# Where the weights of the second projections are split into high and low halves

## The chip, the cores and the metric

The kernel runs on one core of a Trainium2 chip. The metric is the device time of one launch in microseconds (us), median of several runs. The five engines of a core are named as in the profile: PE (TensorE, matrix products; PEld are its weight loads), DVE (VectorE), ACT (ScalarE), POOL (GpSimd) and SP (SyncE, which here issues nearly all transfers).

## The reference

One decoder layer on 8 sequences of 100 tokens, width 1024, all in float32, with a layer normalization after each of three parts:

```
x = layernorm(x + retention(x, Wq, Wk, Wv, Wg, Wo, g_norm_weight))
x = layernorm(x + attention(x, ctx_2048, wq, wk, wv, wo, wk_ctx, wv_ctx, q_norm_w, k_norm_w))
x = layernorm(x + w_down @ (silu(w_gate @ x) * (w_up @ x)))
```

The retention has 8 heads: queries and keys of 128, values and gates of 256, a decaying causal mask in place of a softmax. The attention has 16 query heads on 4 key and value heads of 128; its keys are 722 of the context and the 100 of the sequence itself. The part that the change is about are the second projections, those of the attention's own queries, keys and values:

```
q = rms_norm((x @ wq).reshape(B, L, 16, 128), q_norm_w)
k = rms_norm((x @ wk).reshape(B, L, 4, 128), k_norm_w)
v = (x @ wv).reshape(B, L, 4, 128)
q, k = rope(q), rope(k)
```

## The kernel before, in words

Activations lie with the features on the 128 partitions and the tokens along the free dimension, in two halves of N = 400 tokens (four sequences each). A float32 product is made of three products of float32r numbers: every operand is kept as a high half (a cast on ACT, L67) and a low half (operand minus high half, on DVE, L68), and `mm3` (L85) multiplies high by high, high by low and low by high. A weight tile covers 1024 inputs and 128 outputs: 512 KB raw, 1 MB as two halves.

`load_w` (L70) loads a raw weight into a tile `wst` (3 buffers), and splits it into a tile `w` (4 buffers). `load_ws` (L80) loads a weight that was split earlier: it reads both halves, 1 MB, out of the DRAM tensor `wcd` straight into a tile `w`, and needs neither `wst` nor a split. Both pools serve the whole kernel.

The stages, in order of time:

- The retention (to about 430 us). Head 0 is computed directly, heads 1 to 7 with seven products in place of eight (`seven`, L342). Each head has three units (queries and keys, values, gates), and `in_turn` (L408) interleaves the steps of neighbouring units. A unit loads two raw weights and takes three `w` tiles. After a head's value unit `after_v` (L552) puts the values in place and calls `core` (L475): scores, products with the values, and at its end one of the eight context weights `wc` is loaded, split, and written to `wcd` (L498 to L503), where the later stages find it. After the gate unit `after_g` (L557) calls `gated` (L505), which writes the head's result to the DRAM tensor `o1d`.
- The output projection of the retention, `out_proj` (L216), for one half of the tokens after the other, about 430 to 580 us. Before each half, eight loads of 800 KB bring `o1d` into four `big` tiles (L562), of which there are only four, so the second half's loads wait for the first half's products. It goes through eight blocks m of 128 outputs (in half 0 the first four together), each with two weights of `wo1` and 48 products. After the last block a layer normalization follows.
- The second projections, about 575 to 842 us (L622 to L654). For each of the four key heads kv there are six weights `w2[kv, i]`: four of queries (i = 0 to 3), one of keys (4), one of values (5). They are loaded by L628 with `load_w`, four or two at a time. Each is used for both halves, 24 products of 400 columns for each. A query or key result then passes, on ACT, POOL and DVE: square (L645), the all-reduce over partitions on POOL (L125), the rotation (L133 to L137), the inverse root (L113 to L120), the scaling (L650) and a split (L68), and goes to DRAM (L654). A value result is transposed by PE (L148) after a copy on ACT (L145). Between the weights the keys of the first context sequence are prepared (`context_keys`, L592, which loads from `wcd`).
- The attention over the eight sequences, its output projection, and the feed-forward part.

The accumulators are PSUM banks: three with tag a, four with tag s, one with tag v. PE executes in order. The order of the instructions on each engine is not written by hand: the launch builds the program with `schedule_with_timeline_sim=True` (L1070), by which a planner orders them from the program text, a simulated timeline, and the buffers that are free. SP issues its transfers in that order, each when what it waits for is done.

Of the kernel before, what the change touches and what calls it, by code (L numbers as in the profile page):

```python
# [9 lines left out]
FR = mybir.dt.float32r  # L10
# [6 lines left out]
P = 128  # L17
# [3 lines left out]
KT = D // P  # L21
QT = KT // 2
# [9 lines left out]
NKV = 4  # L32
# [7 lines left out]
def decoder_layer(ctx, tc, xT, cT, w1, wo1, w2, wo2, wc, w3, wd, gw, qw, kw, trig, dec, mask, out):  # L40
    nc = tc.nc
# [14 lines left out]
    def f32(ap):  # L56
        return ap.bitcast(F32)
# [19 lines left out]
            split(w[:, :, c], st[:, c])  # L77
        return w

    def load_ws(i):  # L80
        w = wp.tile([P, 2, KT * P], FR, tag="w", name="w", bufs=4)
        nc.sync.dma_start(out=f32(w), in_=f32(wcd[i]))
        return w

    def mm3(acc, lh, ll, rh, rl, start, stop, chain=False):  # L85
        nc.tensor.matmul(acc, lh, rh, start=start, stop=False, skip_group_check=chain)  # L86
# [70 lines left out]
    zd = dr.tile([2, P, KT, N], F32, name="zd")  # L157
    zd2 = dr.tile([2, P, KT, N], F32, name="zd2")
    wcd = dr.tile([2 * NKV, P, 2, KT * P], FR, name="wcd")
    hd = dr.tile([QT - 1, 7, P, 2, QT, N], FR, name="hd")  # L160
    h3d = dr.tile([4, P, 2, QT, N], FR, name="h3d")

# [50 lines left out]
        return dcy  # L213


    def out_proj(half, w, load_o, res, yp, ybufs, p, make_z, dst, after=None):  # L216

        og = load_o(half)
        y = yp.tile([P, KT, N], F32, tag="y", name="y", bufs=ybufs)
        s1 = p.tile([P, N], F32, tag="s1", name="s1", bufs=2)  # L220
        first = 4 if half == 0 else 1
        for ms in [range(first)] + [[m] for m in range(first, KT)]:
            if half == 1 and KT - 1 in ms:
                early = norm_early(y, s1, p)
            accs = [bank(("aaasaaaa", "sssaaass")[half][m])[:, :N] for m in ms]
            for c in range(2):
                for m, acc in zip(ms, accs):
                    wt = load_w(w[m, c])
                    for k in range(KT):
                        kt = c * KT + k  # L230
                        rh, rl = og(kt)
                        a = acc if len(rh.shape) == 2 else bt(acc)
                        mmw(a, wt, k, rh, rl, kt == 0, kt == 2 * KT - 1)
            for m, acc in zip(ms, accs):
                rs = yp.tile([P, N], F32, tag="rs", name="rs", bufs=2)
                nc.sync.dma_start(out=rs, in_=res[half, :, m])
                if half == 1 and m == KT - 1:
                    nc.vector.tensor_tensor(rs, rs, early[0], ALU.subtract)
                nc.vector.tensor_tensor(y[:, m], acc, rs, ALU.add)
                if half == 0 or m < KT - 1:  # L240
                    add_up(s1, y, m)
        z = make_z(half)
        if half == 0:
            scaled(y, norm_root(y, s1, p), lambda m: dst[half, :, m], z)
        else:
            norm_more(y, early, p, KT - 1)
            norm_late(y, early, p, lambda m: dst[half, :, m], z)
        if after is not None:
            after(half, y)
        return z  # L250
# [171 lines left out]
    with sbuf("l1", 2) as p:  # L422
# [127 lines left out]
                of_qk(half, i, acc)  # L550

        def after_v(h, c):  # L552
            for (half, blk), acc in c:
                of_v(half, blk, acc, (half, blk) == HB[3])
            core(h)

        def after_g(h, c):  # L557
            gated(h, {hb: silu(acc, None if hb == HB[3] else acc) for hb, acc in c})

        in_turn([unit(h, i, then) for h in range(1, NH1) for i, then in ((0, after_qk), (2, after_v), (4, after_g))])  # L560
# [6 lines left out]

    z1pool = sbuf("z1", 4)
    z1p = z1pool.__enter__()
    with sbuf("ln1", 1) as p:  # L570
        z1 = [out_proj(half, wo1, load_o1, xT, p, 2, p, lambda _: [z1p.tile([P, 2, QT, N], FR, tag="z", name="z")
                                                                 for _ in range(2)], zd) for half in range(2)]


    kapool = sbuf("ka", 2, "right")
# [16 lines left out]
    def context_keys(kv):  # L592

        kall = ka.tile([P, 2, SC + T], FR, tag="kall", name="kall")
        wk = load_ws(2 * kv)
        sq = ka.tile([P, SC], F32, tag="ksq", name="ksq", bufs=1)
        ss = ka.tile([P, 6 * P], F32, tag="kss", name="kss", bufs=1)
        row = dr.tile([6, P], F32, tag="row", name="row", bufs=2)
        nc.gpsimd.memset(ss[:, SC:], 1.0)

        def step(hf):
            n, at = SN[hf], slice(hf * SH, hf * SH + SN[hf])
            acc = proj(wk, cz[hf], n)
            nc.scalar.activation(sq[:, at], acc, AF.Square)  # L604
            nc.gpsimd.partition_all_reduce(ss[:, at], sq[:, at], P, RED.add)  # L605
            nc.scalar.activation(kall[:, 0, at], acc, AF.Copy, scale=kws)
            nc.vector.scalar_tensor_tensor(kall[:, 1, at], acc, kws, f32(kall[:, 0, at]), ALU.mult, ALU.subtract)
            if hf:
                nc.sync.dma_start(out=row.rearrange("c p -> (c p)")[None, :], in_=ss[0:1])
        return step, (kall, row)  # L610

    def context_values(kv):

        wv = load_ws(2 * kv + 1)
        vt = ka.tile([P, SC], F32, bufs=1, tag="cvt", name="cvt")
        for hf in range(2):
            copy = nc.scalar.copy if hf == 0 else nc.vector.tensor_copy
# [457 lines left out]
```

## Time and profile before

| | |
|---|---|
| median of 3 runs | 2516.4 us (2514.87 to 2523.12) |
| the profiled execution | 2517.7 us |
| its span, first to last instruction | 2515.9 us |
| PE busy | 2465.4 us |
| DVE busy | 1992.2 us |
| ACT busy | 1343.5 us |
| transfers | 433.96 MB, mean 172 GB/s |

The prediction quotes the page (busy time and share of each engine, then the span in 40 slices whose digits are tenths of busy time), the table by stretches of time, the list of who waited for whom (engine, tile and line that waited, the engine, tile and line that ended the wait, total us, times, longest), and the timeline (start and length in us, engine, line, operation, tiles; in brackets the idle time before it and what ended it). A tile is named by the program's name for it; "w<-wst" is an operation that writes w and reads wst. A line may be that of a helper: all splits of weights stand at L67 and L68. A wait is put down to the releaser that the profile saw last, which need not be the true one.

### The profile page before, as it was taken

The page shows a single profiled execution, that of the slowest core. Times are in us where ns is not written, and L with a number is a line of the kernel's source. Part 1 is how long each engine was busy: PE and PEld are TensorE (multiplying, and loading weights), DVE is VectorE, ACT ScalarE, POOL GpSimd, SP SyncE. Part 2 cuts the span into 40 slices and gives each one's busy share as a digit, 9 for nine tenths or more (in the row PEclk, how much of TensorE's full clock was granted, in tenths as well). Part 3 has the DMA queues.
Part 4 walks back from the last instruction along what each step waited for, and adds up shares of the span by engine and source line. Part 5 has one row for each costly group of instructions (what it writes and reads, how often), then busy time and mean ns, then how long its engine had stood idle before and what let it go on. Part 6 is the DMA issues. An engine that isn't in the chain of part 4 may idle for free.

```text
span 2515.9 us, 37158 instructions
## 1 busy us (share of the span) xinstructions
PE 2465.4 (98%) x14036; PEld 2442.0 (97%) x14036; DVE 1992.2 (79%) x3110; ACT 1343.5 (53%) x2264; POOL 481.2 (19%) x234
## 2 busy tenths in 40 slices
PE   8999999999899999999999999999999999999997
PEld 8999999999899999999999999999999999998997
DVE  7678876568989798899999999866987777666656
ACT  6667676335767565556566566533544544432221
POOL 0111111002645334433433433100000000000000
PEclk9999999999999999999999999999999999999999
DMA  7334445774444654554554554574455445388731
GB/s 240 110 110 127 136 144 187 239 266 148 144 152 133 207 175 142 178 166 151 169 176 144 166 192 135 189 273 152 145 181 192 159 160 167 127 302 311 250 102 53
DMA packets 224450, 433.96 MB, mean 172 GB/s; under 512 B 47338, under 2 KB 168042, under 8 KB 211854
## 3 DMA queue, kind: packets, MB, share of 16 engines
q1 hardware_dynamic: 223118, 427.39, 50.7%
q0 software_dynamic: 1152, 4.19, 1.1%
q8 instruction: 110, 1.80, 0.3%
q14 instruction: 70, 0.57, 0.1%
HBM read 322.18 MB, written 109.35 MB: 172 GB/s over the span
## 4 chain that ended last, share of the span: by engine, by line
PE 89%; DVE 6%; ACT 1%; DMA 1%; issue 1%; SPq 0%; DVEq 0%; ACTq 0%
PE a L88 18%; PE a L86 18%; PE a L87 18%; PE s L88 9%; PE s L87 9%; PE s L86 9%; PE v L88 2%; PE v L86 2%; PE v L87 2%; PE s L491 1%; PE s L688 1%; DVE r L120 1%; DVE r L119 1%; PE s L148 1%; DMA tp<-in_xT 1%
## 5 line engine op out<-in xcount | busy, mean ns | idle before, releaser
L86 PE MATMUL a<-big,w 128*128 128x400 f32 (+2 forms) x1808 | 611.4, 339 | 11.7 <-ACT big L67 7.4
L87 PE MATMUL a<-big,w 128*128 128x400 f32 (+2 forms) x1808 | 611.1, 338 | 0.0
L88 PE MATMUL a<-big,w 128*128 128x400 f32 (+2 forms) x1808 | 609.7, 338 | 0.0
L67 ACT CAST w<-wst 128x1024 fp32r<-128x1024 f32 (+1 forms) x231 | 239.2, 1038 | 389.4 <-PE s L88 130.7
L68 DVE TENSOR_TENSOR w<-wst,w 128x1024 fp32r<-128x1024 f32 (+1 forms) x231 | 281.0, 1218 | 117.0 <-ACT w L67 115.1
L86 PEld LDWEIGHTS a<-big,w 128*128 128x128 f32 x1808 | 341.3, 189 | 13.3 <-ACT big L67 7.7
L87 PEld LDWEIGHTS a<-big,w 128*128 128x128 f32 x1808 | 342.0, 189 | 1.3 <-DVE big L68 0.3
L88 PEld LDWEIGHTS a<-big,w 128*128 128x128 f32 x1808 | 342.0, 189 | 0.9 <-DVE w L68 0.2
L86 PE MATMUL s<-big,w 128*128 128x400 f32 x664 | 230.6, 347 | 0.1
L87 PE MATMUL s<-big,w 128*128 128x400 f32 x664 | 229.2, 345 | 0.0
L88 PE MATMUL s<-big,w 128*128 128x400 f32 x664 | 229.1, 346 | 0.0
L125 POOL PARTITION_ALL_REDUCE ss<-sq x56 | 161.1, 2881 | 336.3 <-DMA zd<-y 167.0
L605 POOL PARTITION_ALL_REDUCE kss<-ksq x64 | 173.2, 2706 | 116.4 <-ACT ksq L604 115.7
L86 PE MATMUL a<-z,w 128*128 128x400 f32 x488 | 168.6, 346 | 8.0 <-ACT r L118 4.3
L88 PE MATMUL a<-z,w 128*128 128x400 f32 x488 | 169.4, 348 | 0.7 <-DVE w L68 0.7
L87 PE MATMUL a<-z,w 128*128 128x400 f32 x488 | 169.4, 347 | 0.0
L87 PE MATMUL s<-z,w 128*128 128x400 f32 x400 | 139.1, 348 | 2.4 <-DVE z L68 2.4
L86 PE MATMUL s<-z,w 128*128 128x400 f32 x400 | 139.9, 350 | 0.0
L88 PE MATMUL s<-z,w 128*128 128x400 f32 x400 | 139.4, 348 | 0.0
L722 ACT ACTIVATE s<-s,rk 128x400 f32<-128x400 f32 x160 | 87.7, 591 | 91.9 <-DVE sm L742 65.5
L86 PEld LDWEIGHTS s<-big,w 128*128 128x128 f32 x664 | 124.6, 188 | 1.4 <-ACT w L67 0.4
L87 PEld LDWEIGHTS s<-big,w 128*128 128x128 f32 x664 | 124.6, 188 | 1.1
(330 smaller groups left out, 5650.9 us busy)
## 6 DMA issues: line engine op xcount, KB each, us to landing
wst<-in_w SPq DMA_DIRECT2D x135, 512.0 KB
w<-wcd SPq DMA_DIRECT2D x64, 1024.0 KB
wst<-in_wo SPq DMA_DIRECT2D x64, 512.0 KB
hd<-h SPq DMA_DIRECT2D x12, 1400.0 KB
wst<-in_wd SPq DMA_DIRECT2D x64, 256.0 KB
big<-o1d SPq DMA_DIRECT2D x16, 800.0 KB
qd<-d SPq DMA_DIRECT2D x32, 400.0 KB
q<-qd SPq DMA_DIRECT2D x32, 400.0 KB
```

The lines of the kernel that those rows point to most:

```text
L67: nc.scalar.copy(hi, src)
L68: nc.vector.tensor_tensor(lo, src, f32(hi), ALU.subtract)
L86: nc.tensor.matmul(acc, lh, rh, start=start, stop=False, skip_group_check=chain)
L87: nc.tensor.matmul(acc, lh, rl, start=False, stop=False, skip_group_check=chain)
L88: nc.tensor.matmul(acc, ll, rh, start=False, stop=stop, skip_group_check=chain)
L119: nc.vector.scalar_tensor_tensor(q, ss, eps, q, ALU.add, ALU.mult)
L120: nc.vector.scalar_tensor_tensor(q, q, 3.0, r, ALU.subtract, ALU.mult)
L125: nc.gpsimd.partition_all_reduce(y, x, P, op)
L148: nc.tensor.transpose(tr[0:T, b * P:(b + 1) * P], vt[:, b * T:(b + 1) * T], ident)
L491: nc.tensor.matmul(bt(o)[:, b], vv[:, b * P:(b + 1) * P], pf[:, b], start=True, stop=True)
L605: nc.gpsimd.partition_all_reduce(ss[:, at], sq[:, at], P, RED.add)
L722: nc.scalar.activation(sc, sp, AF.Copy, scale=rk[:, c:c + 1])
```

## The change

The 24 weights `w2[kv, i]` are no longer split where they are used. A new DRAM tensor `w2d` (24 MB) holds both halves of each. A new function `split_ahead` takes the next of them from a list, loads and splits it with `load_w`, and writes the 1 MB tile to `w2d`. It is called at the head of `after_v` and of `after_g` in the retention's heads 1 to 7 (14 calls), and in the retention's output projection by way of a new argument `beside` of `out_proj`, once after the products of each block: in half 0 for blocks 4 to 7 and in half 1 for blocks 0 to 5, until the list is empty (10 calls). The second projections read the halves with `load_ws`, which is given the source instead of an index.

```diff
-    def load_ws(i):
+    def load_ws(src):
         w = wp.tile([P, 2, KT * P], FR, tag="w", name="w", bufs=4)
-        nc.sync.dma_start(out=f32(w), in_=f32(wcd[i]))
+        nc.sync.dma_start(out=f32(w), in_=f32(src))
         return w
+
+    ahead = [(kv, i) for kv in range(NKV) for i in range(6)]
+
+    def split_ahead():
+
+        kv, i = ahead.pop(0)
+        nc.sync.dma_start(out=f32(w2d[kv, i]), in_=f32(load_w(w2[kv, i])))
...
+    w2d = dr.tile([NKV, 6, P, 2, KT * P], FR, name="w2d")
...
-    def out_proj(half, w, load_o, res, yp, ybufs, p, make_z, dst, after=None):
+    def out_proj(half, w, load_o, res, yp, ybufs, p, make_z, dst, after=None, beside=None):
...
                         mmw(a, wt, k, rh, rl, kt == 0, kt == 2 * KT - 1)
+            if beside is not None:
+                beside(half, ms[-1])
             for m, acc in zip(ms, accs):
...
         def after_v(h, c):
+            split_ahead()
             for (half, blk), acc in c:
...
         def after_g(h, c):
+            split_ahead()
             gated(h, {hb: silu(acc, None if hb == HB[3] else acc) for hb, acc in c})
...
+    def weights_ahead(half, m):
+        if ahead and (half == 1 or m >= QT):
+            split_ahead()
...
-        wk = load_ws(2 * kv)
+        wk = load_ws(wcd[2 * kv])
...
-        wv = load_ws(2 * kv + 1)
+        wv = load_ws(wcd[2 * kv + 1])
...
-                ws = [load_w(w2[kv, i]) for i in range(i0, i1)]
+                ws = [load_ws(w2d[kv, i]) for i in range(i0, i1)]
```

More of the change, by code (lines that the diff above doesn't have):

```diff
@@ L569, in decoder_layer @@
     z1p = z1pool.__enter__()
+    def weights_ahead(half, m):
+        if ahead and (half == 1 or m >= QT):
+            split_ahead()
     with sbuf("ln1", 1) as p:
         z1 = [out_proj(half, wo1, load_o1, xT, p, 2, p, lambda _: [z1p.tile([P, 2, QT, N], FR, tag="z", name="z")
-                                                                 for _ in range(2)], zd) for half in range(2)]
+                                                                 for _ in range(2)], zd, None, weights_ahead)
+              for half in range(2)]
     kapool = sbuf("ka", 2, "right")
```

## The prediction

> **What bounds the kernel now.** First the page: its busy shares, and its slices in time.
>
> ```profile
> PE 2465.4 (98%) x14036; PEld 2442.0 (97%) x14036; DVE 1992.2 (79%) x3110; ACT 1343.5 (53%) x2264; POOL 481.2 (19%) x234
> ...
> PE   8999999999899999999999999999999999999997
> DVE  7678876568989798899999999866987777666656
> ```
>
> TensorE (PE) does not idle for more than 51 us of 2515.9 us. A change that takes nothing from PE can win only where PE waits or runs slowly. So I read the table by stage next (columns: stretch, its length, busy time and number of instructions of PE, PEld, DVE, ACT and POOL, granted clock, DMA share, GB/s). The stretches are the retention, the output projection up to its second half, the load burst between the halves, the second half, the normalization and start of the second projections, and these in two parts.
>
> ```profile
> 110.00:430.00 320.00, 319.50 (x1919) 317.34 (x1919) 247.05 (x368) 219.23 (x350) 37.73 (x18) 1.00 0.43 137
> 430.00:504.00 74.00, 74.00 (x419) 74.00 (x419) 37.79 (x47) 30.11 (x39) 6.16 (x4) 1.00 0.75 240
> 504.00:530.00 26.00, 24.63 (x133) 23.74 (x132) 14.22 (x22) 9.47 (x15) 0.00 (x0) 1.00 0.93 368
> 530.00:575.00 45.00, 44.74 (x247) 44.41 (x246) 27.91 (x41) 15.86 (x22) 0.00 (x0) 1.00 0.61 188
> 575.00:616.00 41.00, 37.70 (x190) 36.17 (x191) 36.97 (x60) 23.74 (x42) 7.51 (x2) 0.96 0.51 157
> 616.00:720.00 104.00, 91.68 (x479) 89.55 (x479) 101.59 (x142) 73.59 (x142) 55.14 (x19) 0.95 0.42 136
> 720.00:842.00 122.00, 121.11 (x680) 120.34 (x679) 110.56 (x158) 87.16 (x167) 64.94 (x26) 1.00 0.46 157
> ```
>
> In the retention and the output projection PE is full and VectorE (DVE) is at 77% and about 55%. From 616 to 720 it is the reverse: DVE is busy 101.6 of 104 us, and PE does 479 instructions, where from 720 to 842 it does 680 in 122 us, 5.57 per us. At that rate 479 take 86 us, so **this stretch loses 18 us**: 12.3 us idle, the rest at a lowered clock and in stretched products. The same table for the DVE instructions on tile w alone gives the splits of the weights there (length, DVE busy and count):
>
> ```profile
> 616.00:720.00 104.00, 13.44 (x10) 0.95 0.42 136
> 720.00:842.00 122.00, 12.87 (x10) 1.00 0.46 157
> ```
>
> The list of what PE waited for between 604 and 720 (total, times, longest):
>
> ```profile
> PE a L86 <- ACT r L118: 4.3, 1, 4.3
> PE s L148 <- ACT vt L145: 3.5, 2, 2.8
> PE a L86 <- DMA w<-wcd: 2.5, 1, 2.5
> PE s L87 <- DVE z L68: 2.4, 1, 2.4
> PE a L86 <- ACT w L67: 1.4, 1, 1.4
> PE a L88 <- DVE w L68: 0.7, 1, 0.7
> ```
>
> The first is put down to ACT, but the timeline shows DVE's L135 read of an accumulator end at 635.3 us and PE go on at 635.44: all banks were full and DVE was behind. Four splits (at 617.7, 622.5, 625.1 and 631.6 us; the third took 2.51 us where others take 1.22) stand ahead of it on DVE. After this wait ten products come 0.33 us apart instead of 0.18. The waits for L145 are DVE's backlog as well: ACT copies vt only after casts that waited for DVE's L650. Two waits are for splits themselves, one is for a load, and one for the normalization's last split.
>
> **What is removed.** 24 splits (ACT cast 1.04 us, DVE subtraction 1.22 us each) leave the second projections: 4 before 590 us, 10 in the DVE-bound stretch, 10 after 720.
> - 616 to 720: DVE loses 13.4 us of 101.6 and comes to 88.2, against 86 us of PE work. Of PE's 18.1 us, the load wait at 677 stays (2.5 us idle and about 1.5 us of slow clock: eleven products at 0.30 apart). That leaves 14.1; DVE can give back 13.4. Both engines are then nearly level, so some waits must come back: I take 2 us off. **Gain 11.4 us**; bounds 2.1 us (only the two waits that name a split) and 18.1.
> - Before 616: PE waits 1.1 us at 575.9 for the cast of a w2 weight, which goes. Splits at 582.7 and 588.0 (2.45 us) stand in DVE's queue among the normalization's steps, and PE then waits 2.4 us for its z. I take half: 1.2 us. **Gain 2.3 us**; bounds 0 and 5.4 (1.1, 2.4 and 1.9 of slow clock).
> - After 720: DVE loses 12.9 us, but PE is busy 121.1 of 122. Gain nothing.
>
> **What is added: 14 pieces in the retention** (load 512 KB, cast, subtraction, write 1 MB; two in each of seven heads). A head takes 53 us. DVE gets 2.4 us more on about 41 and ACT 2.1 on 36, PE's 319.5 of 320 us cover both. Each piece also keeps a raw buffer (of 3) and a w buffer (of 4) until its write has landed. The nearest rows: the context weight that the head already splits and writes (cast at 261.05, second ACT copy at 264.62, write issued at 265.69, next DMA on it at 270.3: 9 us of a buffer), and in 110 to 430 PE waited 0.5 us in all. So nothing is the lower bound. For the upper: with one buffer held, three serve the products, and the scarcest weight has two products, 24 x 0.182 = 4.4 us, from release to use; cast and subtraction take 2.3 us, and the subtraction's wait for its cast was 27.9 us over 11 times between 160 and 420, so 2.5 us: 0.4 us late, times 14, 6 us. The nearest row says nothing, so I take **1.5 us**.
>
> On SP each write waits for its subtraction, and later raw loads, o1d stores and wc loads are queued behind it. The loads are issued early (five between 267 and 295), and ACT and DVE waited under 4 us for raw weights from 160 to 420, so I price this within the 1.5 us.
>
> **10 pieces in the output projection.** A block m takes 48 products, 8.7 us, and loads 1 MB of weights and 0.2 MB of residue; with 1.5 MB more it moves 2.7 MB, 310 GB/s, and the trace reaches 410 to 429 GB/s from 507 to 524 us. DVE and ACT have room (27.9 and 15.9 of 45 us). The tight place is the burst: 6.4 MB of o1d for the second half can be asked for only as the first half's tiles come free (issues from 504.45 to 511), and PE wants the last of them 8.7 us after 512.3. A piece's 1.5 MB is 3.7 us there. Bounds nothing and 5.4 us (3.7 and 1.7 of clock); I take **2 us**, since a part falls before the burst. The page "DMA: Bandwidth & Descriptors" of the Trainium skill (Queues, rings and completion order) has each DMA engine take the descriptors of one issuing queue in ring order. This speaks against the change: a write issued ahead of the o1d loads holds them all up. By it this term would be 3.7 us and not 2; no row here shows such a write.
>
> **1 MB loads in place of a 512 KB load and a split.** The row is the load at 677: issued on SP at 670.82, landed 6.2 us later.
>
> ```profile
> 670.82 0.38 SPq L82 DMA_DIRECT2D w<-wcd  x1
> ...
> 677.00 0.67 PE L86 MATMUL a<-big,w 128*128 128x362 f32 x1 [2.46 <-DMA w<-wcd]
> ```
>
> The second weight of a pair takes a buffer that comes free 4.4 us before the pair ahead ends, and is wanted 4.4 us into its own: 8.7 us against 6.2. It fits, unless SP is 2.5 us late. Bounds: nothing, and 8 us (two more waits of 4 us, at the other places where a key weight is wanted with a pair). I take **1 us**. The same page (Anatomy of one DMA) fits 2.0 us and bytes over 436 GB/s, an estimate of 4.4 us for 1 MB; the row has 6.2 with other traffic beside it, and by the page's figure this term would be nothing.
>
> **Sum.** 11.4 + 2.3 - 1.5 - 2 - 1 = 9.2 us. The profiled execution took 2517.7 us (span 2515.9 and 1.8 around it), so it would take 2508.5. The median of the three runs, 2516.4, lies 1.3 us lower: 2507.2, **2507 us**, 0.4% faster.
>
> **Rivals.**
> 1. *DVE's chain stays the bound.* All-reduces on POOL fill 52 of the 104 us, and DVE operations beside them stretch (L136 takes 0.56 us as a rule and up to 2.17). Without splits DVE still runs level with PE, and each stretched step delays a bank. For it: 88 against 86 us. Against: from 720 on the all-reduces are as dense (56.6 in 122 us), splits are there too, and PE is full. Half of the 11.4 us returns: 2516.4 - 5.7 - 2.3 + 4.5 = 2513 us.
> 2. *Slower: the w buffers of the retention.* At the end of each head's v unit a piece and the context weight come together and hold two of four buffers for 8 to 9 us. The product after them then waits: the longest wait of a subtraction for its cast is 5.8 us; with 2.3 less the 4.4 of cover, PE stops for 3.7. Times seven: 26 us, and 2516.4 - 13.7 + 3 + 26 = 2532; half of that, 13 us, gives 2519; the middle is 2525. It outweighs the gain from 1.5 us a head. Against: the heads' own PE work on scores (about 6 us) lies just there, and the same place now costs nothing.
> 3. *The loads take the place of the splits:* SP holds the 1 MB loads up behind stores that wait for DVE, and the waits of PE change only their name. 8 us instead of 1 there, 3.7 in the burst: 2516.4 - 13.7 + 1.5 + 3.7 + 8 = 2516 us; the change then does not do what it says.
>
> **Chances.** Forecast 0.55 (own range 2499 to 2512), rival 1 0.18, rival 2 0.15, rival 3 0.12. 0.3%, 7.5 us, is about what a measurement of this kernel can tell from no change. Of the forecast 0.45 lies below 2508.9 and 0.10 above; rival 1 gives 0.05 and 0.13; rival 3 counts as no change with 0.07 and as slower with 0.05; rival 2 is slower. So 0.50 faster, 0.30 the same, 0.20 slower. The range leaves 0.1 out at each side: 2498 (a gain of 18) to 2525.
>
> **What would show it.** In the profile after: the busy DVE share from the start of the second projections falls under nine tenths, the waits for L118 and L145 go, and the first 479 PE instructions there take some 90 us. Waits of PE for loads into w tell rival 3. The retention still takes 53 us a head; more, with PE waiting for w, is rival 2. PE waiting for big at the start of the second half is the burst. The forecast is wrong if PE's lost time in that stage stays above 9 us, or the retention and output projection lose more than 8.

## The result, and the profile after

The changed kernel takes **2543.2 us** (median of four runs, 2541.3 to 2545.0) against 2515.6 us for the kernel before on the same chip: a ratio of 1.0103, interval 1.0091 to 1.0115. It is 27.6 us slower, where 9.2 us faster was predicted. The profiled execution took 2543.8 us, with a span of 2542.0; that is 26.1 us over the span before.

The page after, busy time and slices:

```profile
PE 2474.5 (97%) x14036; PEld 2444.0 (96%) x14036; DVE 1992.4 (78%) x3110; ACT 1346.1 (53%) x2264; POOL 470.1 (18%) x234
...
PE   8999999889999999999999999999999999999997
DVE  7777777565987789989989989866987777666755
```

Each engine has exactly as many instructions as before, so the splits have only moved; the transfers grew from 434 to 484 MB. In PE's row the eight at the eleventh slice of before is a nine, and there are two new eights, slices 8 and 9 (445 to 572 us), where DVE has a five and a six. The time went where DVE was not the bound.

The table by stage after (columns as in the prediction; the stretches are the heads up to the scores of head 3, the heads from there to those of head 7, the last part of the retention with the first half of the output projection, and its second half):

```profile
112.00:213.00 101.00, 101.00 (x605) 100.66 (x605) 82.08 (x121) 70.28 (x113) 13.82 (x6) 1.00 0.53 171
213.00:445.00 232.00, 221.18 (x1295) 214.93 (x1293) 174.30 (x258) 155.25 (x244) 24.36 (x12) 0.99 0.57 189
445.00:542.50 97.50, 88.50 (x473) 85.53 (x473) 51.53 (x60) 39.92 (x49) 6.24 (x4) 0.96 0.89 310
542.50:620.00 77.50, 67.89 (x346) 65.30 (x344) 46.50 (x67) 29.25 (x40) 0.00 (x0) 0.94 0.92 334
```

The kernel before in stretches that answer to the last three, with about the same PE instructions:

```profile
213.00:430.00 217.00, 217.00 (x1311) 215.89 (x1311) 167.03 (x247) 149.83 (x240) 25.51 (x12) 1.00 0.45 144
430.00:514.00 84.00, 82.63 (x464) 82.04 (x464) 42.62 (x53) 32.35 (x42) 6.16 (x4) 1.00 0.77 253
514.00:578.00 64.00, 62.87 (x344) 61.95 (x343) 40.16 (x61) 24.08 (x35) 0.00 (x0) 1.00 0.67 230
```

From 112 to 213 us PE has no idle time in the new kernel, though three pieces are written in that stretch (at 127.6, 159.8 and 183.0 us). From 213 us on PE idles for 10.8 us where it did not idle at all, then for 9.0 where it was 1.4, then for 9.6 where it was 1.1, at a lower granted clock each time (0.99, 0.96 and 0.94 for 1.00).

The second projections after, cut at the same counts of PE instructions as before (the 190 ahead of the stretch that the prediction calls DVE-bound, its 479, and the rest):

```profile
618.13:654.00 35.87, 35.87 (x190) 34.70 (x191) 32.12 (x55) 20.78 (x38) 7.23 (x2) 1.00 0.65 224
654.00:748.00 94.00, 89.17 (x479) 88.30 (x478) 92.04 (x132) 64.76 (x132) 54.20 (x19) 0.96 0.56 201
748.00:876.80 128.80, 127.79 (x719) 126.95 (x718) 102.60 (x155) 81.30 (x164) 63.36 (x27) 1.00 0.59 209
```

Before, the middle part is the prediction's line from 616 to 720 us; the other two are:

```profile
576.30:616.00 39.70, 37.28 (x190) 35.74 (x189) 35.71 (x58) 22.92 (x41) 7.51 (x2) 0.96 0.51 156
720.00:850.50 130.50, 127.73 (x718) 126.66 (x716) 113.39 (x165) 89.16 (x173) 66.70 (x27) 1.00 0.50 164
```

So before they took 39.7, 104.0 and 130.5 us. The 479 instructions take 94 us, so 10 us are gained there. DVE is still busy 92 of these 94 us, so it runs level with PE and is not below nine tenths.

PE's waits after, from 618 to 880 us:

```profile
PE a L93 <- DMA w<-wcd: 2.5, 1, 2.5
PE a L93 <- ACT r L123: 2.4, 1, 2.4
...
PE a L93 <- DMA w<-w2d: 0.8, 1, 0.8
...
```

The lines named here stand 7 further down than before (L86 is L93, L118 is L125, L145 and L148 are L152 and L155). The waits for a split are gone, and the one for the copy of vt fell from 3.5 to 0.2 us. The wait of 4.3 us that was put down to L118 has a successor of 2.4 us, put down to L123, the step ahead of L125 in the same inverse root. The load from `wcd` still costs 2.5 us; the new loads from `w2d` cost 0.8.

**A ledger by marks on PE** shows each run of this study by the same five marks: the mean time between the first scores of heads 4, 5, 6 and 7; the start of the first scores of head 7; from there to the first product of the mean in the first half's normalization; from there to the same product of the second half; from there to the first transposes of the keys of the first context sequence (before at 850.5 us). One profiled execution each, in us. The part behind the last mark takes 1665 us in the two kernels, and within about 4 us of that in the others.

| kernel | a head | head 7 at | to the mean, half 0 | second half | second projections | span |
|---|---|---|---|---|---|---|
| before | 52.8 | 421.8 | 90.5 | 64.0 | 274.2 | 2515.9 |
| after | 57.4 | 438.9 | 101.7 | 77.6 | 258.7 | 2542.0 |
| `free` | 52.8 | 421.4 | 90.5 | 63.7 | 258.4 | 2499.1 |
| `ret14` | 57.1 | 437.0 | 100.4 | 63.7 | 261.5 | 2527.9 |
| `proj10` | 52.8 | 421.8 | 90.8 | 79.7 | 267.1 | 2522.0 |
| `ret14_late` | 54.2 | 426.8 | 102.5 | 63.7 | 261.0 | 2518.9 |
| `ret14_wcsplit` | 54.4 | 428.5 | 90.5 | 63.7 | 260.4 | 2506.3 |
| `ret14_nowrite` | 53.0 | 421.5 | 95.0 | 63.7 | 260.4 | 2504.2 |
| `before_wcsplit` | 53.9 | 425.2 | 91.0 | 64.0 | 273.2 | 2522.8 |
| `ret7_v` | 52.8 | 420.3 | 90.7 | 63.7 | 268.5 | 2505.5 |
| `ret7_g` | 52.8 | 420.3 | 90.5 | 63.7 | 270.2 | 2508.2 |
| `ret14_writeonly` | 52.8 | 437.3 | 90.5 | 63.7 | 260.5 | 2515.9 |
| `ret14_poolq` | 56.6 | 444.1 | 100.0 | 63.7 | 260.3 | 2531.3 |
| `ret14_ownraw` | 52.8 | 422.6 | 94.0 | 63.8 | 260.8 | 2504.1 |
| `ret14_ownw8` | 52.8 | 424.6 | 92.6 | 63.7 | 261.6 | 2506.5 |
| `burst4` | 52.8 | 421.3 | 91.1 | 74.3 | 272.4 | 2527.8 |
| `proj8` | 52.8 | 424.1 | 91.8 | 63.9 | 277.1 | 2522.2 |
| `spots13` | 52.8 | 425.9 | 90.5 | 63.7 | 261.5 | 2510.3 |
| `spots14` | 52.8 | 420.6 | 91.2 | 68.4 | 260.9 | 2506.5 |

After against before: +17.1 up to head 7, +11.2 from there through the first half, +13.5 in the second half, -15.5 in the second projections. The sum is +26.3; the spans differ by 26.1.

### The profile page after: what moved, and what is told of

Same layout as the page of the kernel before. It is cut to its first block, busy times and chain, and to the rows that moved or that the text cites. A ratio compares the mean times of both kernels' runs of the same rounds, so it can differ in the third digit from the quotient of the medians.

```text
span 2542.0 us, 37231 instructions
## 1 busy us (share of the span) xinstructions
PE 2474.5 (97%) x14036; PEld 2444.0 (96%) x14036; DVE 1992.4 (78%) x3110; ACT 1346.1 (53%) x2264; POOL 470.1 (18%) x234
## 4 chain that ended last, share of the span: by engine, by line
PE 79%; DVE 10%; DMA 5%; ACT 3%; issue 2%; SPq 1%; POOL 0%; DVEq 0%; ACTq 0%; POOLq 0%
PE a L95 16%; PE a L93 16%; PE a L94 16%; PE s L95 8%; PE s L94 8%; PE s L93 8%; DMA wst<-in_w 2%; DVE r L127 2%; PE v L95 2%; PE v L93 2%; PE v L94 2%; DVE w L68 1%; DVE t L667 1%; DVE r L126 1%; PE s L705 1%
## 5 line engine op out<-in xcount | busy, mean ns | idle before, releaser
L93 PE MATMUL a<-big,w 128*128 128x400 f32 (+2 forms) x1808 | 613.3, 340 | 23.3 <-ACT w L67 12.0
L93 PEld LDWEIGHTS a<-big,w 128*128 128x128 f32 x1808 | 342.3, 189 | 28.0 <-ACT w L67 14.5
L93 PE MATMUL s<-big,w 128*128 128x400 f32 x664 | 232.7, 350 | 3.6 <-ACT w L67 2.1
L622 POOL PARTITION_ALL_REDUCE kss<-ksq x64 | 165.6, 2587 | 113.6 <-ACT ksq L621 112.9
L93 PE MATMUL a<-z,w 128*128 128x400 f32 x488 | 168.3, 345 | 4.3 <-ACT r L123 2.4
L93 PE MATMUL s<-z,w 128*128 128x400 f32 x400 | 138.6, 347 | 0.0
L93 PEld LDWEIGHTS s<-big,w 128*128 128x128 f32 x664 | 126.1, 190 | 6.2 <-ACT w L67 2.8
```

## The experiments

Each is the changed kernel with the edit shown, unless it says otherwise. All planner decisions are made anew in each, so an edit can move other instructions too. The medians stand against that of the kernel before on the same chip.

### The parts alone: free, ret14, proj10

`free` makes no pieces and reads the halves of context weights in place of those of `w2`:

```diff
-            split_ahead()
...
-                ws = [load_ws(w2d[kv, i]) for i in range(i0, i1)]
+                ws = [load_ws(wcd[(6 * kv + i) % 8]) for i in range(i0, i1)]
```

> Leaves out all 24 pieces; the second projections read halves of context weights in place of their own (so other numbers, the same work). It measures the gain alone. In the changed kernel the way from the last normalization's mean product of the output projection to the first context transposes took 258.7 us, before 274.2: a gain of 15. Both theories (late buffers and engines; late transfers) expect 2515.6 - 15 = 2500 us, plus or minus 3. If 1 MB loads cost more where nothing else was moved, over 2505.

Measured: 2501.7 us, ratio 0.9943 (0.9928 to 0.9958). The second projections take 258.4 us, as in the kernel after, and nothing else changes. So the gain is what the forecast said it was; the pieces eat it.

`ret14` makes only the retention's 14 pieces, and the other ten weights are split where they are used:

```diff
-        if ahead and (half == 1 or m >= QT):
+        if False:
...
-                ws = [load_ws(w2d[kv, i]) for i in range(i0, i1)]
+                ws = [load_ws(w2d[kv, i]) if 6 * kv + i < 14 else load_w(w2[kv, i]) for i in range(i0, i1)]
```

> Only the 14 pieces in the retention; the last 10 weights are split where they are used, after PE is full there. In the changed kernel heads 4 to 7 took 4 to 5 us longer each, 17 us in all, and the gain in the second projections lies in the first 14 weights. Theory A (the retention has no room for the pieces: buffers, ACT and DVE order): 2515.6 + 17 - 14 = 2519, and more if the stop at the start of the output projection (5 us and a cold clock) stems from head 7's piece: up to 2526. Theory B (only the transfers of the output projection are the trouble): 2505.

Measured: 2532.1 us, 1.0065 (1.0050 to 1.0080). Up to head 7 it loses 15.3 us and from there through the first half 9.9, together 25 of the 28 us that the kernel after loses there. The second projections gain 12.7 with 14 weights, where 24 gain 15.5.

`proj10` makes only ten pieces, in the output projection:

```diff
-    ahead = [(kv, i) for kv in range(NKV) for i in range(6)]
+    ahead = [(kv, i) for kv in range(NKV) for i in range(6)][:10]
```

with both calls in the retention left out, and the other 14 weights split where they are used.

> Only the 10 pieces in the output projection, with the first 10 weights; the other 14 are split where they are used. Second half of the output projection cost 13.4 us in the changed kernel, the end of its first half 3 or so. Gain of 10 weights: the 4 before the stretch and 6 of the 10 in it, 8 to 10 us. Theory A (retention is the trouble): 2508 or less. Theory B (transfers full in the output projection): 2515.6 + 15 - 9 = 2522.

Measured: 2523.4 us, 1.0031 (1.0021 to 1.0041). The first half costs 0.3 us, the second half 15.7. The pieces beside blocks 4 to 7 of the first half and the ones of the second half are equal in number to within two, so it is the place that decides.

### What two pieces in a head run out of

What the heads wait for in the kernel after is the splitting itself. PE's waits from 213 to 445 us, of which there were none from 213 to 430 before:

```profile
PE a L93 <- ACT w L67: 6.2, 5, 2.0
PE a L95 <- DVE w L68: 1.9, 4, 1.1
...
```

ACT, one step back, waits for the raw weight. First the kernel before, then after:

```profile
ACT w L67 <- DMA wst<-in_w: 1.0, 1, 1.0
```

```profile
ACT w L67 <- DMA wst<-in_w: 18.5, 7, 5.8
```

One step further back is SP, which issues the raw loads. In the kernel after, `load_w`'s load at L76 (here the piece's) waits for the transfer in which POOL adds the raw context weight into `wcd` (the longest 14.1 us): that transfer holds one of the three raw buffers.

```profile
...
SPq L76 <- DMA wcd<-wst: 51.6, 4, 14.1
```

The timeline of SP around one such place, with a piece's raw load (L76) 12.9 us after the write of the context weight (L512):

```profile
333.48 0.33 SPq L512 DMA_DIRECT2D wcd<-w  x1
346.35 0.33 SPq L76 DMA_DIRECT2D wst<-in_w  x1
```

SP issues nothing else from 333.8 to 346.3. Such a wait existed before, too (38.4 us over four times, for L333); it cost PE nothing then, and ACT waited for raw weights for 1.0 us in all.

Behind head 7 a weight of the output projection comes late as well. PE's longest stop there, in the kernel after, is for a cast, and ACT had waited for that weight's raw load until 473.4 us:

```profile
474.52 0.70 PE L93 MATMUL a<-big,w 128*128 128x400 f32 x1 [5.39 <-ACT w L67]
```

Several causes fit: the order on SP, the writes' traffic, the raw buffers, and the w buffers. The next runs take them one by one.

`ret14_late` is `ret14` with `split_ahead()` called after `core` and after `gated` instead of ahead of them.

```diff
         def after_v(h, c):
-            split_ahead()
...
                 core(h)
+                split_ahead()
```

> As the kernel with 14 pieces in the retention, but each piece stands at the end of its step in the program text (after core, after gated) instead of ahead of it. If the planner's order is what hurts (the piece's cast and subtraction ahead of the score work on ACT and DVE), the heads shrink by more than half of their 4 to 5 us: 8 us or more under the kernel with 14 pieces. If it is the buffers or the transfers, within 3 us of it.

Measured: 2520.7 us, 1.0025 (1.0014 to 1.0035). A head takes 54.2 us in place of 57.1, so the place in the text is worth 3 us a head, two thirds of what the pieces cost there; but the loss after head 7 is the full 12. By the expectation this is the outcome for the planner's order, 11 us under `ret14` with the same number of buffers. Order matters and doesn't cure. It also sets how long a piece holds its buffers, so this run doesn't separate the two.

`ret14_wcsplit` is `ret14` with the context weight split like every other (no POOL transfer holding a raw buffer), and `before_wcsplit` has that edit alone, on the kernel before:

```diff
-            w = wp.tile([P, 2, KT * P], FR, tag="w", name="w", bufs=4)
-            st = load_raw(wc[h])
-            nc.scalar.copy(w[:, 0], st)
-            nc.scalar.activation(w[:, 1], f32(w[:, 0]), AF.Copy, scale=-1.0)
-            nc.sync.dma_start(out=f32(wcd[h]), in_=f32(w))
-            nc.gpsimd.dma_start(out=f32(wcd[h])[:, 1], in_=st, accum_op=ALU.add)
+            nc.sync.dma_start(out=f32(wcd[h]), in_=f32(load_w(wc[h])))
```

> The kernel with 14 pieces in the retention, with one more edit: the context weight of each head is split like the others (one cast, one subtraction on DVE) and written once, without the second ACT copy and without POOL's accumulating transfer, which in that kernel keeps one of three raw buffers; SP's raw load of a piece waited for that transfer 52.7 us in 4 heads, with the next loads queued behind it. Theory A1 (that raw buffer is what stops SP): heads 4 to 7 lose their 4 us, 10 to 15 us under 2532. Theory A2 (the order of work on ACT and DVE alone): DVE gets more work at the same place, so the same or slower than 2532.

> The kernel before with only the other edit of the third-last experiment group: the context weights split with one cast and one subtraction, written once, no accumulating transfer on POOL. It tells whether that edit is worth anything by itself. PE waited 0.5 us in the retention of the kernel before, so 2516 plus or minus 3. If it is worth 10 us or more by itself, the 24 us that it gained beside the 14 pieces say less about the pieces.

Measured: `ret14_wcsplit` 2508.4 us, 0.9964 (0.9953 to 0.9974); `before_wcsplit` 2523.7 us, 1.0033 (1.0021 to 1.0046). The same edit costs 8 us without the pieces, where no change was expected, and saves some 24 beside them: a head falls from 57.1 to 54.4 (`before_wcsplit` has 53.9), and the loss after head 7 vanishes. Of the 6.9 us that the profiled execution of `before_wcsplit` is longer, 3.4 lie before head 7 (1.1 us a head) and 3.9 behind the last mark, where the program text is the same. With the edit a raw buffer comes free after the subtraction, and isn't kept for POOL's transfer. That this holding time is part of the cause fits, but the edit also changes the work of DVE and ACT; so the buffers are tried by themselves below.

`ret14_nowrite` makes the pieces (load and split) but doesn't write them; the 14 weights are read from halves of context weights instead:

```diff
-        nc.sync.dma_start(out=f32(w2d[kv, i]), in_=f32(load_w(w2[kv, i])))
+        load_w(w2[kv, i])
```

> The kernel with 14 pieces in the retention, but the pieces' write is left out; the first 14 weights of the second projections are read from the context weights' halves (other numbers, the same work). If the 1 MB writes are the trouble (transfers, or w buffers kept until they land): 8 us or more under 2532. If it is the raw buffer, or the order of ACT and DVE: within 4 us of 2532.

Measured: 2505.0 us, 0.9949 (0.9934 to 0.9964). A head takes 53.0 us. Loads, casts and subtractions alone cost next to nothing in the heads (4.5 us remain after head 7). So it is the write, by its traffic, its place on SP, or the w buffer that it keeps.

`ret14_writeonly` is the opposite: no load, no split, and a write of 1 MB from a resident tile in its place; the 14 weights are again read from halves of context weights.

```diff
-        nc.sync.dma_start(out=f32(w2d[kv, i]), in_=f32(load_w(w2[kv, i])))
+        nc.sync.dma_start(out=f32(w2d[kv, i]).rearrange("p l c -> p (l c)"), in_=f32(still[0]))
```

> The 14 pieces reduced to their write: 1 MB from a resident tile to the new DRAM tensor, no raw load, no split, no buffer; the first 14 weights of the second projections are read from context weights' halves (other numbers, the same work). If the write traffic ahead of the raw loads in the queue is enough: last scores 8 us or more later than 425.9. If it takes the buffers, or the wait of SP for the split: within 3 us of 425.9, and near 2503 in all.

Measured: 2518.7 us, 1.0016 (1.0005 to 1.0026). The total misleads: this kernel loses 16.6 us before head 1's scores, where PE waits for ACT's casts at the start. In the heads the period is 52.8, and from 213 to 430 us PE waits for nothing. The writes' traffic costs the heads nothing.

`ret14_poolq` lets POOL issue the write, so that SP no longer waits for the piece's subtraction:

```diff
-        nc.sync.dma_start(out=f32(w2d[kv, i]), in_=f32(load_w(w2[kv, i])))
+        nc.gpsimd.dma_start(out=f32(w2d[kv, i]), in_=f32(load_w(w2[kv, i])))
```

> The kernel with 14 pieces in the retention, with the pieces' writes issued by POOL in place of SP: the same buffers, splits and bytes, but SP does not wait for a piece's subtraction, and the raw loads do not stand behind the write in SP's own queue. Theory Q (raw weights come late because SP holds them behind the piece's write, then behind its blocked raw load): last scores 8 us or more earlier than the 441.2 us of that kernel. Theory B (the raw and w buffers that two pieces a head keep): within 4 us of 441.2.

Measured: 2531.9 us, 1.0063 (1.0045 to 1.0081), as `ret14`; a head takes 56.6 us, and head 7 begins 7 us later still. Taking the write out of SP's order doesn't help. It is no clean test, since POOL now waits for the subtraction in its own order (31.6 us ahead of the write at 335.9 us); but `ret14_ownraw` and `ret14_ownw8` below keep the write on SP and lose nothing in the heads, so its place there is not enough to cause the loss.

`ret7_v` keeps only the piece at the value step (7 weights), `ret7_g` only that at the gate step:

```diff
         def after_g(h, c):
-            split_ahead()
```

> Seven pieces only, one at the head of each value step, where the head's context weight follows. If a piece costs because it meets the context weight (buffers, and SP held up by the accumulating transfer): heads 4 to 7 lose about 4 us each, as with both, and the last scores start 12 to 17 us later than before (425.9 us). If it is the number of pieces: half of that, 6 to 8 us.

> Seven pieces only, one at the head of each gate step, with no context weight beside it. If the meeting with the context weight is the trouble: the last scores start within 3 us of the kernel before (425.9 us). If it is the number of pieces: 6 to 8 us later.

Measured: `ret7_v` 2509.5 us, 0.9974 (0.9962 to 0.9985); `ret7_g` 2510.7 us, 0.9981 (0.9970 to 0.9992). Both have heads of 52.8 us and lose nothing after head 7. `ret7_v` fits neither branch of its expectation, and it rules out the one that `ret7_g` fits, the meeting with the context weight. One piece a head is free, wherever it stands; in `ret7_v` it even meets the context weight at the end of the value unit, which rival 2 took for the cause. Two cost 4 to 5 us a head from head 3 on, so the cost here is a threshold and not a sum. ACT waits for raw weights in `ret7_v` as well (10.7 us over six times, 213 to 430 us), and PE for nothing: half of the waits of `ret14` are still covered.

`ret14_ownraw` gives the pieces a raw buffer of their own in place of a share of the three, and `ret14_ownw8` a tile of their own for the halves in place of a share of the four. Space for it is taken from single tiles of the retention (one buffer in place of more for pf, t2, r0, and in the second also for r1, with eight in place of ten for tp).

```diff
-        nc.sync.dma_start(out=f32(w2d[kv, i]), in_=f32(load_w(w2[kv, i])))
+        st = lp[0].tile([P, KT * P], F32, tag="ast", name="ast", bufs=1)
+        w = wp.tile([P, 2, KT * P], FR, tag="w", name="w", bufs=4)
+        nc.sync.dma_start(out=st, in_=w2[kv, i])
+        split(w, st)
+        nc.sync.dma_start(out=f32(w2d[kv, i]), in_=f32(w))
```

In `ret14_ownw8` it is the other way round (`st` from the shared three, `w` as a tile `aw` with one buffer).

> The kernel with 14 pieces in the retention, but the pieces load into a raw buffer of their own (4 KB a partition, paid for by one buffer instead of two for three small tiles of the retention), so that the three shared ones serve the units and the context weight as before. If the raw buffers that the pieces take are the trouble: last scores at 430 us or earlier, against 441.2. If it is the w buffers: within 4 us of 441.2.

> The kernel with 14 pieces in the retention, but the pieces split into a w buffer of their own (8 KB a partition, paid for by one buffer instead of two for four small tiles and eight instead of ten for another), so that the four shared ones serve the units and the context weight as before. If the w buffers that the pieces keep until their write has landed are the trouble: last scores at 430 us or earlier, against 441.2. If it is the raw buffers: within 4 us of 441.2, or later if the smaller tiles are missed.

Measured: `ret14_ownraw` 2508.3 us, 0.9968 (0.9949 to 0.9988); `ret14_ownw8` 2506.5 us, 0.9956 (0.9937 to 0.9976). Both bring the head back to 52.8 us with two pieces in each head, and leave 2 to 3.5 us of the 10 after head 7. ACT's casts of the weights that the products want hardly wait for raw loads any more (not at all and 0.5 us); in `ret14_ownraw` ACT waits 5.5 us over four times for the write of a piece, which still keeps a shared w buffer. SP's wait for the POOL transfer is still there (33.7 us over four times in `ret14_ownw8`, for the piece's load), so that wait alone is not the price. The line of `ret14` from 213 to 430 us, and that of `ret14_ownw8`, in which such waits are left for the piece's own tile `aw` alone, where nothing but the piece is late:

```profile
ACT w L67 <- DMA wst<-in_w: 20.9, 9, 6.5
```

```profile
ACT aw L67 <- DMA wst<-in_w: 11.4, 5, 3.3
```

So the shared buffers are what two pieces use up at these places. One more of either kind is enough to bring the heads back; which of the two runs out first, these runs don't separate, since a w buffer that comes free late holds the cast back, and with it the raw buffer.

### The place in the output projection: burst4 and proj8

In the kernel after, the loads of `o1d` for the second half are issued with a piece between them. SP from 538 to 548 us:

```profile
538.47 0.85 SPq L577 DMA_DIRECT2D big<-o1d  x2
539.45 0.35 SPq L90 DMA_DIRECT2D w2d<-w  x1
541.38 0.33 SPq L76 DMA_DIRECT2D wst<-in_w  x1
542.69 2.23 SPq L577 DMA_DIRECT2D big<-o1d  x2
```

A 1 MB write and a 512 KB load stand between two `o1d` loads and the next two, and the loads of the next weights of `wo1` follow at 547.9. PE then stops three times by 570 us (idle time ahead of the product in brackets):

```profile
558.38 0.45 PE L93 MATMUL s<-big,w 128*128 128x400 f32 x1 [1.44 <-DMA big<-o1d]
565.10 0.45 PE L93 MATMUL s<-big,w 128*128 128x400 f32 x1 [2.10 <-ACT w L67]
569.10 0.70 PE L95 MATMUL s<-big,w 128*128 128x400 f32 x1 [3.36 <-DVE w L68]
```

Only the first is `o1d` itself; the longer two are weights of `wo1` that came late. The rule of the Trainium skill that the prediction weighed ("DMA: Bandwidth & Descriptors", Queues, rings and completion order: each DMA engine takes one queue's descriptors in ring order) has this direction, and spoke rightly against the change. The price that the prediction set for it, 3.7 us, was far too small: from 530 to 575 us the DMA share is 1.00, and PE's three stops there come to 6.9 us.

`burst4` makes four pieces around the burst alone (block 7 of half 0, blocks 0 to 2 of half 1), `proj8` eight away from it (blocks 4 to 6, and 3 to 7), both none in the retention:

```diff
-        if ahead and (half == 1 or m >= QT):
+        if ahead and (m == KT - 1 if half == 0 else m <= 2):
```

```diff
-        if ahead and (half == 1 or m >= QT):
+        if ahead and (m in (4, 5, 6) if half == 0 else m >= 3):
```

> Four pieces only, around the burst of o1d loads: block 7 of the first half, blocks 0 to 2 of the second. With 10 pieces the way between the two halves' mean products took 79.7 us, with 8 pieces away from the burst 63.9, before 64.0. If the place is what costs: 74 us or more. If the number of pieces (10 against 8): under 68 us.

> 8 pieces in the output projection, none near the burst of o1d loads: blocks 4 to 6 of the first half, 3 to 7 of the second. With 10 pieces the way from the first half's mean product to the second's early mean took 79.7 us, before 64.0, and all the waits of PE lie in the first 35 us of it. If the burst is the trouble: 64 to 67 us, and 2515.6 + 2 - 8 = 2509. If ten or eight pieces overload the transfers wherever they lie: 72 us or more, 2516 or more.

Measured: `burst4` 2529.6 us, 1.0054 (1.0036 to 1.0072); `proj8` 2517.7 us, 1.0003 (0.9994 to 1.0013). Four pieces at the burst cost 10.3 us in the second half; eight away from it cost nothing there. The burst from 503 to 545 us, first in the kernel before, then in `burst4`, then in `proj8`:

```profile
503.00:545.00 42.00, 40.63 (x221) 39.74 (x220) 29.24 (x48) 18.14 (x30) 0.00 (x0) 1.00 0.83 306
```

```profile
503.00:545.00 42.00, 33.54 (x163) 30.92 (x162) 30.48 (x48) 18.71 (x30) 0.00 (x0) 0.92 1.01 376
```

```profile
503.00:545.00 42.00, 40.63 (x221) 39.53 (x220) 27.64 (x42) 19.61 (x30) 0.00 (x0) 1.00 0.89 341
```

In 42 us PE does 163 instructions with a DMA share of 1.01, and 221, as many as before, with one of 0.89. `proj8` gained nothing in the second projections of its profiled execution, though it takes eight splits out of them, and its median shows no gain either, where 7 us were expected. That execution, at 2523.9 us, was the longest of its runs, 6 us over the median, so its ledger is not read to the last microsecond. `burst4` gained 1.8 there with the first four, `proj10` 7.1 with the first ten.

### Versions from these results: spots13 and spots14

`spots13` makes two pieces in each of heads 1 to 3 (where PE had no idle time in the kernel after, up to the scores of head 3), none later, and seven in the output projection away from the burst. `spots14` makes one in each of seven heads, at the value step, and the same seven (the edit shown is that of `spots14`):

```diff
         def after_g(h, c):
-            split_ahead()
...
-        if ahead and (half == 1 or m >= QT):
+        if ahead and (m in (4, 5, 6) if half == 0 else 3 <= m <= 6):
```

> 13 pieces only where none has cost anything so far: in heads 1 to 3 (six), in blocks 4 to 6 of the first half (three) and 3 to 6 of the second (four); the other 11 weights are split where they are used, nearly all where PE is full anyway. If costs belong to places: the gain of 12 to 14 us with 0 to 3 us of cost, 2502 to 2506. If a piece costs wherever it stands: 2512 or more.

> 14 pieces, one a head in the retention (at the value step; seven of them left the heads at 52.8 us) and seven in the output projection away from the burst. The heads should stay at 52.8 us, the two ways of the output projection at 86 and 64 us, and the second projections gain as with the first 14 weights, 12 to 13 us: 2503, 2501 to 2506. If the count of pieces matters beyond the places: 2508 or more.

Measured: `spots13` 2510.3 us, 0.9974 (0.9962 to 0.9985); `spots14` 2504.1 us, 0.9952 (0.9939 to 0.9966), 10.9 us faster than the kernel before on the same chip. It beats both kernels, and has the lowest median here that does the whole work, though its interval doesn't separate it from `ret14_ownw8` (0.9937 to 0.9976); `free`, which has no pieces, reached 0.9943. `spots13` missed its expectation of 2502 to 2506: it lost one step of 58 us between the scores of heads 3 and 4, in which the two pieces of head 3 are written (at 214.8 and 239.6 us). The same two pieces of heads 1 and 2 cost nothing. `spots14` lost 4.4 us in the second half, where `spots13`, with the same blocks, lost nothing. Its profiled execution, 2508.3 us, was the longest of five and 4.2 over the median, so this loss need not be in the others; why it came, is open.

## Why the prediction was wrong

**The gain was right**, in mechanism and nearly in size: 11.4 + 2.3 - 1 = 12.7 was predicted, 15.5 measured. Its parts, by the cut at equal counts: 10.0 in the DVE-bound stretch (11.4 was taken), 3.8 before it (2.3), 1.7 after it (nothing less the loads' 1). The 1 MB loads made PE wait 0.8 us once. The fit of the Trainium skill that the prediction set beside them ("DMA: Bandwidth & Descriptors", Anatomy of one DMA; 4.4 us for 1 MB, an estimate) is given there for transfers that GpSimd issues, and these are issued by SP. The prediction said also that DVE would fall under nine tenths there. It didn't: DVE gave back 9.6 us in place of 13.4 and ran level with PE, 92 of 94 us, as rival 1 said, without the 5.7 us that rival 1 priced for it. Some 8 of the 18 us stayed lost: PE waited 2.4 us for L123 and 2.5 for the load from `wcd`, and the granted clock of the stretch was 0.96.

**The step that failed is "14 pieces in the retention", taken at 1.5 us with an upper bound of 6.** It cost 17.1 us in the heads and 11.2 from head 7 through the first half, 28 in all. The bound held one buffer away and let three serve the products, one piece at a time, with the loads in early; and the nearest row, one context weight a head at no cost, was read as a price of nothing for two pieces more. It also let a piece keep its raw buffer until its write has landed, though the write reads the w buffer alone; the transfer that does keep a raw buffer is the context weight's on POOL, and the row for it, SP's 38.4 us of waiting in the kernel before, was not weighed. What the runs show in its place: that row and one piece more are still free (52.8 us a head in `ret7_v` and `ret7_g`), and two pieces beside it, from head 3 on, exhaust the shared buffers (a buffer of their own, raw or w, brings 52.8 back). Then raw loads are issued late (SP's L76 waited 51.6 us behind the POOL transfer), casts come late (ACT waited 18.5 us for raw weights, where it had waited 1.0), and PE stops 13 times, for 10.9 us in all and 2.0 at the longest. Where in its step a piece stands decides much of the size (54.2 us a head in `ret14_late`). The sentence "The loads are issued early ... so I price this within the 1.5 us" took as given what the change would take away: early loads need free buffers.

**The second such step is "10 pieces in the output projection", taken at 2 us.** It cost 13.5 us, all in the second half. The place was named rightly and the mechanism was half right: `o1d` came late, but PE's two longer stops were for weights of `wo1`. The bound of 5.4 us held one piece's bytes at full rate, 3.7 us, and the clock after one stop. But four pieces stand around the burst, and these four alone cost 10.3 us in `burst4`; the transfers were already busy there for 0.93 of the time, and later loads, those of `wo1`, came late too.

With the three terms at their measured sizes the sum is 2507 + (28.3 - 1.5) + (13.5 - 2) - (15.5 - 12.7) = 2542.5 us; 2543.2 was measured. The ledger's parts add up to the span, so this is no test of the causes; it does show that nothing changed behind the last mark. The first term takes in all that was lost up to the end of the first half, of which `ret14` alone shows 25.

**The rivals.** Rival 2 named the resource, or one of its two kinds, and a price of 13 to 26 us in the retention; 28 was measured. Its mechanism, the meeting of one piece with the context weight, is refuted by `ret7_v`; two pieces a head are needed. At 0.15 it got too little for a change that doubles what the shared buffers have to carry: the argument against it ("the same place now costs nothing") is no argument about a load that isn't there yet. Its own times, 2519 to 2532 us, stay under the measured one because the output projection was left at 2 us in them, and the stated range ended at their middle, 2525. Rival 3 is refuted in the second projections: PE's waits for loads into w in the second projections were 3.3 us in all, 2.5 of them old.

**What stays open.** Why heads 1 and 2 carry two pieces each for nothing and the heads from 3 on don't; which of the two kinds of buffer runs out first; how much of the cost is the planner's order, which every edit here changes, and how much the number of buffers; why the context weight's plain split costs 8 us in `before_wcsplit`; which weights among the 24 bring most of the gain (by the ledger seven brought 4 to 6 us, 13 to 14 brought 13, 24 brought 15.5, and the first eight of `proj8` none). More shared buffers were not tried: the pieces' own tiles fitted only after other tiles had given up buffers.

## What to carry to other kernels

Work moved "into the shade" of a full PE is not free because engines have time left: count the buffers that it holds and for how long, beside what already holds them at that place, and be ready for a threshold in place of a price per piece (here one piece a head was free, and two cost 4 to 5 us). Keep added transfers out of a stretch that the DMA engines already fill (here 0.93 of the time, and four pieces cost 10.3 us). And price each edit alone before the sum: a gain of 15.5 us with 24 pieces came out as 27.6 us slower, and one of 13.3 us with 14 pieces at other places as 10.9 us faster.

## What was not expected of the hardware

**After two short stops within 3.4 us the clock was halved.** In the kernel after PE waited 0.52 and 1.08 us between 336.2 and 339.6 us, and was busy for 1.80 of these 3.40 us. Ten products after that came 0.33 us apart in place of 0.18. The table of those stretches (granted clock third from the right):

```profile
336.20:339.60 3.40, 1.80 (x8) 1.17 (x8) 3.11 (x3) 1.82 (x3) 2.60 (x1) 0.98 0.54 228
339.60:343.00 3.40, 3.40 (x11) 3.36 (x12) 3.26 (x5) 0.00 (x0) 0.88 (x1) 0.52 0.48 48
```

The page "TensorE: Matmul & The Clock Gate" of the Trainium skill (Part 1) puts the low clock after an idle window of about 3.4 us. Here 3.4 us that were idle for less than half were enough, and the measurement decides. It is no sharp bound: from 561.30 to 564.71 us PE was busy for 1.70 of 3.41 us, and the granted clock stayed at 1.00 in the next 3.39 us. Where the clock does fall, a stop has a second price: ten products at 0.15 us more are 1.5 us, about as much as the two waits together.

**A DVE subtraction of 1.22 us took 2.62 us** (336.71 to 339.33) while an all-reduce ran on POOL from 336.52 to 339.12. It was the subtraction that PE waited for at 339.39.

**Fourteen writes of 1 MB cost the heads nothing** when they came from a resident tile (`ret14_writeonly`, 52.8 us a head). The same writes from the shared w buffers, with the loads and splits ahead of them, cost 4.3 us a head (`ret14`, 57.1).
